# Message product: one weight block, both column halves of adj, two open accumulators

## Chip, cores, metric

The kernel runs on one NeuronCore of a Trainium2 chip. The metric is the device time of one execution in microseconds; lower is better. Three executions of the kernel before took 1776.67, 1779.15 and 1781.03 us; the median, 1779.15, is the time before.

## What is computed

The input is x, 16 graphs of 1024 nodes with 128 features, and one adjacency matrix adj of 1024 by 1024 that holds zeros and ones. Layer 0 is graph attention with a layer norm; layer 1 is a gated graph network of five steps with a layer norm. The part that matters here is the step of layer 1, cut from the reference:

```python
def step(h, _):
    m_in = jnp.einsum('nm,bmd->bnd', in_matrix, h)    # in_matrix = out_matrix = adj
    m_out = jnp.einsum('nm,bmd->bnd', out_matrix, h)
    av = jnp.concatenate([m_in, m_out], axis=-1)
    u3 = h @ u3_w.T + u3_b
    z = jax.nn.sigmoid(av @ w3_w.T + w3_b + u3)
    r = jax.nn.sigmoid(av @ w4_w.T + w4_b + u3)
    hv = jnp.tanh(av @ w5_w.T + w5_b + (r * h @ u5_w.T + u5_b))
    h = (1.0 - z) * h + z * hv
    return (h, None)
```

Both matrices are adj, so the kernel computes the message m = adj @ h once for each graph and step and folds the two halves of each weight into one (`wm`).

## The kernel before

Everything of layer 1 is held transposed: 128 features on the partitions, 1024 nodes along the row. A row of 1024 is handled in two halves of 512 (`HALF`)[...].

The message product is `s1` (lines 395 to 415). It multiplies the node states, in chunks of 128 nodes, with the rows of adj. The state `hN` is kept as the sum of two float32r tiles (index w, a rounded part and the rest), so 8 chunks times 2 parts give 16 terms for each half. The state is the weight (stationary) operand, a block of 128 by 128; adj is the moving operand, 512 columns. For half 0 all 16 terms accumulate into one bank `pm`, ScalarE copies it to SBUF as `m` (line 413), then the same 16 weight blocks are gone through again for half 1 with the other bank. That makes 32 matmuls on line 405 and two copies for each graph and step, and 16 x 5 = 80 graph steps in all.

The gates follow in `s2`: for each half one matmul with u3 (`pu`, line 423), one for r and one for z (`pr`, `pz`, line 428), each a float32 matmul that TensorE runs in two passes, with additions on VectorE and sigmoids on ScalarE. `s3` computes the candidate (`pv`, lines 443 and 444), tanh on ScalarE and the update on VectorE. `s4` transposes the new state (`pt_h`, line 255) and splits it into the two parts of `hN` (lines 459 and 460). Layer 0 is `f1` to `f4`; its line 365 uses adj and the same pool of accumulators, as `po`.

The graphs are interleaved by hand. A loop over k runs, in this order, the gates of unit k-1, the product of unit k, the candidate of unit k-1, the transposes of unit k-2 and one part of layer 0; so another unit's matmuls stand between a product and the gates that read it. The framework places the instructions on each engine's queue by the order of the source, as a planner that works with estimated times sees them ready, and adds the semaphores; the order in the trace can therefore differ from the source. Each engine then runs its queue in order.

PSUM has eight banks: two in `ps_acc` (used by `pm` and `po`), four in `ps_g` (gates), two in `ps_t` (transposes).

A second network for an adj that isn't zeros and ones is compiled in and skipped in these runs.

Of the kernel before, what the change touches and what calls it, by code (L numbers as in the profile page):

```python
# [8 lines left out]
F32 = mybir.dt.float32  # L9
# [6 lines left out]
P = 128  # L16
N = 1024
HALF = 512
NC = N // P
# [7 lines left out]
def kernel(  # L27
# [41 lines left out]
    nc = tc.nc  # L69
# [61 lines left out]
    def network(binary, pools):  # L131


        def pool(name, bufs, space=None):
            kw = {} if space is None else {"space": space}
            return pools.enter_context(tc.tile_pool(name=f"{name}{int(binary)}", bufs=bufs, **kw))
# [14 lines left out]
        ps_acc = pool("ps_acc", 2, PS)  # L151
# [114 lines left out]
        h0T, hT, hN, y0 = {}, {}, {}, {}  # L266
# [128 lines left out]

        def s1(b, s):
            m = []
            for half in range(2):
                pm = ps_acc.tile([P, HALF], F32, tag="acc", name=f"pm_{b}_{s}_{half}")
                if binary:  # L400
                    terms = [(hN[b][:, w, c, :], c) for c in range(NC) for w in range(2)]
                else:
                    terms = [(hN[b][:, c, :], c) for c in range(NC)]
                for i, (lhs, c) in enumerate(terms):
                    nc.tensor.matmul(  # L405
                        pm,
                        lhs,
                        adj[:, c, half * HALF : (half + 1) * HALF],
                        start=(i == 0),
                        stop=(i == len(terms) - 1),  # L410
                    )
                mt = mp.tile([P, HALF], F32, tag="m", name=f"m_{b}_{s}_{half}")
                nc.scalar.copy(mt, pm)  # L413
                m.append(mt)
            S[b, s] = {"m": m}

# [61 lines left out]
        for k in range(-5, last + 3):  # L478
            at(s2, k - 1)
            at(s1, k)  # L480
            at(s3, k - 1)
            at(s4, k - 2)
            b, phase = divmod(k + 5, 5)
            if b < B:
                stage_ = (f1, None, f2, f3, f4)[phase]
                if stage_ is not None:
                    stage_(b)
            if binary and 20 <= k < 20 + NC:
                look_at(k - 20)
            if binary and k == 20 + NC:  # L490
                find_flag()
# [54 lines left out]
```

## Time and profile before

| what | value |
|---|---|
| median of three executions | 1779.15 us |
| profiled span | 1776.1 us |
| TensorE matmul busy | 1694.1 us, 95% |
| VectorE busy | 1069.2 us, 60% |
| ScalarE busy | 823.1 us, 46% |
| matmul records of line 405 | 2560, 653.6 us busy |
| weight loads of line 405 | 2560, 481.4 us busy |
| copies of line 413 | 160, 580 ns each |

PE is TensorE's matmuls, PEld its weight loads, which can run beside a matmul; DVE is VectorE, ACT ScalarE, POOL GpSimd. Busy time is the time in which at least one instruction of the row was open. Matmuls are pipelined: the record of one is its latency, longer than the distance from its start to the next one's start. A row's last column is the idle time of the engine just ahead of these instructions, with what ended it after the arrow.

### The profile page before, as it was taken

What the parts mean: (1) busy time and instruction counts of PE and PEld (TensorE: products, weight loads), DVE (VectorE), ACT (ScalarE), POOL (GpSimd) and SP (SyncE); (2) the same over time, 40 slices, a digit from 0 to 9 for tenths busy, and PEclk for the clock granted to TensorE, in tenths of its full rate; (3) what the DMA queues carried; (4) which work ended last, traced back from release to release, by engine and by line L of the source; (5) the groups of instructions that cost most, each with busy time, mean ns of one, the idle gap of its engine ahead of it and who ended that gap; (6) DMA issues with size and microseconds to landing.
All of it is one profiled execution on the core that took longest, in us unless ns stands there. A gap on an engine that the chain in (4) does not pass through costs nothing.

```text
span 1776.1 us, 17218 instructions
## 1 busy us (share of the span) xinstructions
PE 1694.1 (95%) x6212; PEld 1053.3 (59%) x6212; DVE 1069.2 (60%) x2486; ACT 823.1 (46%) x1430; POOL 243.6 (14%) x196
## 2 busy tenths in 40 slices
PE   3689999999999999999999999999999999999995
PEld 2445666666666666666666666566666666666562
DVE  4586464746656475665747656474675747565555
ACT  3146363554636345463634546354463634544442
POOL 3640101102020020201002010110202001020101
PEclk8799999999999999999999999999999999999998
DMA  5110000000000000000000000000000000000000
GB/s 170 48 48 1 13 1 12 12 13 12 1 12 13 12 13 13 1 13 13 13 12 12 13 1 12 13 13 12 13 1 0 13 0 13 1 12 0 13 0 25
DMA packets 22412, 27.06 MB, mean 15 GB/s; under 512 B 1328, under 2 KB 18096, under 8 KB 22320
## 3 DMA queue, kind: packets, MB, share of 16 engines
q1 hardware_dynamic: 21376, 23.27, 4.2%
q10 hardware_dynamic: 576, 2.10, 0.3%
q8 instruction: 50, 0.82, 0.2%
q0 software_dynamic: 368, 0.53, 0.1%
q14 instruction: 42, 0.34, 0.1%
HBM read 17.50 MB, written 8.39 MB: 15 GB/s over the span
## 4 chain that ended last, share of the span: by engine, by line
PE 85%; DVE 8%; POOL 3%; DMA 2%; ACT 1%; issue 1%; SPq 0%; POOLq 0%; DVEq 0%; ACTq 0%
PE pm L405 33%; PE po L365 8%; PE pz L428 7%; PE pv L444 7%; PE pu L423 7%; PE pr L428 7%; PE pv L443 7%; PE pt_h L255 2%; DVE hv L448 2%; PE ptt L276 2%; PE pe L297 2%; PE ph L343 1%; DVE hv L447 1%; PE po L357 1%; DVE hN L460 1%; POOL zero L217 1%
## 5 line engine op out<-in xcount | busy, mean ns | idle before, releaser
L405 PE MATMUL pm<-adj,hN 128*128 128x512 f32 x2560 | 653.6, 411 | 1.4 <-DVE hN L460 1.1
L405 PEld LDWEIGHTS pm<-adj,hN 128*128 128x128 f32 x2560 | 481.4, 189 | 154.0 <-issue 33.5
L447 DVE TENSOR_TENSOR hv<-hv,h1T 128x512 f32<-128x512 f32 x128 | 88.1, 688 | 293.1 <-ACT hv L446 293.1
L425 ACT ACTIVATE u<-pu,bias 128x512 f32<-128x512 f32 x160 | 109.9, 687 | 192.2 <-PE pu L423 187.5
L430 DVE TENSOR_TENSOR r<-pr,u 128x512 f32<-128x512 f32 x160 | 108.5, 678 | 135.8 <-PE pr L428 124.0
L413 ACT COPY m<-pm 128x512 f32<-128x512 f32 x160 | 91.4, 580 | 196.4 <-PE pm L405 196.4
L444 PE MATMUL pv<-r,u 128*128 128x512 f32 x320 | 163.7, 594 | 7.5 <-DVE r L433 7.5
L446 ACT ACTIVATE hv<-pv,b 128x512 f32<-128x512 f32 x160 | 110.1, 688 | 125.8 <-PE pv L444 125.6
L428 PE MATMUL pz<-m,wm 128*128 128x512 f32 x320 | 167.4, 605 | 0.2 <-DVE r L430 0.2
L443 PE MATMUL pv<-m,wm 128*128 128x512 f32 x320 | 162.9, 592 | 1.4 <-DVE r L430 1.4
L428 PE MATMUL pr<-m,wm 128*128 128x512 f32 x320 | 163.6, 593 | 0.0
L431 ACT ACTIVATE r<-r,bias 128x512 f32<-128x512 f32 x160 | 114.5, 716 | 99.2 <-DVE r L430 99.1
L350 POOL TENSOR_TENSOR h<-full,h 128x512 fp32r<-128x512 f32 x32 | 40.5, 1265 | 795.3 <-ACT h L349 795.3
L431 ACT ACTIVATE z<-z,bias 128x512 f32<-128x512 f32 x160 | 115.2, 720 | 67.8 <-DVE z L430 66.1
L365 PE MATMUL po<-att,h 128*128 128x512 f32 x256 | 115.7, 604 | 24.8 <-DVE h L344 24.8
L423 PE MATMUL pu<-h1T,u 128*128 128x512 f32 x256 | 130.9, 593 | 0.0
L448 DVE TENSOR_TENSOR hv<-hv,z 128x512 f32<-128x512 f32 x160 | 116.8, 737 | 2.3
L430 DVE TENSOR_TENSOR z<-pz,u 128x512 f32<-128x512 f32 x160 | 109.0, 681 | 2.4 <-PE pz L428 2.3
L444 PEld LDWEIGHTS pv<-r,u 128*128 128x128 f32 x320 | 60.1, 189 | 83.1 <-issue 65.2
L451 POOL TENSOR_TENSOR h1T<-h1T,h0T 128x512 f32<-128x512 f32 x32 | 45.4, 1418 | 440.9 <-DVE h1T L449 414.9
L428 PEld LDWEIGHTS pz<-m,wm 128*128 128x128 f32 x320 | 55.6, 189 | 80.7 <-issue 36.6
L365 PEld LDWEIGHTS po<-att,h 128*128 128x128 f32 x256 | 49.3, 194 | 87.3 <-issue 78.4
(105 smaller groups left out, 2012.0 us busy)
## 6 DMA issues: line engine op xcount, KB each, us to landing
xt<-in_x_dram SPq DMA_DIRECT2D x16, 512.0 KB, 3.2
out_dram<-o SPq DMA_DIRECT2D x16, 512.0 KB, 3.2
look<-in_adj_dram SPq DMA_DIRECT2D x8, 512.0 KB, 3.3
a<-in_adj_dram ACTq DMA_DIRECT2D x4, 512.0 KB, 4.3
a<-in_adj_dram SPq DMA_DIRECT2D x4, 512.0 KB, 3.5
w<-in_L_gnn_w_w_dram POOLq DMA_DIRECT2D x3, 128.0 KB, 7.5
u<-in_L_gnn_u_w_dram POOLq DMA_DIRECT2D x2, 64.0 KB, 7.7
wot<-L_gnn_others_weight_dram SPq DMA_DIRECT2D x1, 64.0 KB, 3.3
```

The source lines that it names most:

```text
L365: nc.tensor.matmul(po, lhs, rhs, start=False, stop=(i == len(terms) - 1))
L405: nc.tensor.matmul(pm, lhs, adj[:, c, half * HALF : (half + 1) * HALF], start=(i == 0), stop=(i == len(terms) - 1),)
L423: nc.tensor.matmul(pu, u3, h, start=True, stop=True)
L425: nc.scalar.activation(u, pu, AF.Identity, bias=bias[:, 3:4], scale=1.0)
L428: nc.tensor.matmul(pg, wm[:, j, :], st["m"][half], start=True, stop=True)
L430: nc.vector.tensor_tensor(g, pg, u, ALU.add)
L431: nc.scalar.activation(g, g, AF.Sigmoid, bias=bias[:, j : j + 1], scale=1.0)
L443: nc.tensor.matmul(pv, wm[:, 2, :], st["m"][half], start=True, stop=False)
L444: nc.tensor.matmul(pv, u5, st["r"][half], start=False, stop=True)
L446: nc.scalar.activation(hv, pv, AF.Tanh, bias=b5, scale=1.0)
L447: nc.vector.tensor_tensor(hv, hv, h, ALU.subtract)
L448: nc.vector.tensor_tensor(hv, hv, st["z"][half], ALU.mult)
```

## The change

The two loops of `s1` change places. Both accumulators are taken at the start; for each of the 16 weight blocks the matmul for half 0 is followed at once by the one for half 1, and the two copies come after all 32 matmuls. It is meant to let two matmuls in a row use one weight block. The number of matmuls and copies, their shapes and the order in which each accumulator sums its terms stay the same.

```diff
         def s1(b, s):
             m = []
-            for half in range(2):
-                pm = ps_acc.tile([P, HALF], F32, tag="acc", name=f"pm_{b}_{s}_{half}")
-                if binary:
-                    terms = [(hN[b][:, w, c, :], c) for c in range(NC) for w in range(2)]
-                else:
-                    terms = [(hN[b][:, c, :], c) for c in range(NC)]
-                for i, (lhs, c) in enumerate(terms):
+            pms = [ps_acc.tile([P, HALF], F32, tag="acc", name=f"pm_{b}_{s}_{h}") for h in range(2)]
+            if binary:
+                terms = [(hN[b][:, w, c, :], c) for c in range(NC) for w in range(2)]
+            else:
+                terms = [(hN[b][:, c, :], c) for c in range(NC)]
+            for i, (lhs, c) in enumerate(terms):
+                for half in range(2):
                     nc.tensor.matmul(
-                        pm,
+                        pms[half],
                         lhs,
                         adj[:, c, half * HALF : (half + 1) * HALF],
                         start=(i == 0),
                         stop=(i == len(terms) - 1),
                     )
+            for half in range(2):
                 mt = mp.tile([P, HALF], F32, tag="m", name=f"m_{b}_{s}_{half}")
-                nc.scalar.copy(mt, pm)
+                nc.scalar.copy(mt, pms[half])
                 m.append(mt)
             S[b, s] = {"m": m}
```

## The prediction

> **What bounds the kernel now.** I read the busy rows first, then the stretches, then who waits for whom on TensorE, then the order of time around one message product.
>
> ```profile
> PE 1694.1 (95%) x6212; PEld 1053.3 (59%) x6212; DVE 1069.2 (60%) x2486; ACT 823.1 (46%) x1430; POOL 243.6 (14%) x196
> ```
>
> TensorE (PE) has work 95% of the span, and no other engine is above 60%. Cut into stretches (columns: length, busy us and instruction counts of PE, PEld, DVE, ACT, POOL, then granted clock, DMA share, GB/s):
>
> ```profile
> 0.00:100.00 100.00, 51.43 (x164) 31.47 (x165) 55.25 (x151) 29.10 (x55) 47.05 (x37) 0.80 0.30 102
> 200.00:1690.00 1490.00, 1486.15 (x5482) 926.53 (x5482) 904.69 (x2096) 716.95 (x1244) 162.84 (x138) 1.00 0.03 9
> 1690.00:1776.00 86.00, 64.79 (x224) 38.08 (x222) 44.99 (x102) 30.15 (x48) 9.52 (x8) 0.92 0.05 13
> ```
>
> In the middle 1490 us TensorE idles 3.9 us, at full granted clock. The idle is at the ends: 48.6 us in the first 100, 21.2 us in the last 86. So in the middle the time is the number of matmuls times their pace, and nothing else; removing waits there can bring at most those 3.9 us. The list of TensorE's waits for the middle stretch says the same: its largest entry is 2.1 us.
>
> The row to change is the largest of that engine:
>
> ```profile
> L405 PE MATMUL pm<-adj,hN 128*128 128x512 f32 x2560 | 653.6, 411 | 1.4 <-DVE hN L460 1.1
> L405 PEld LDWEIGHTS pm<-adj,hN 128*128 128x128 f32 x2560 | 481.4, 189 | 154.0 <-issue 33.5
> L413 ACT COPY m<-pm 128x512 f32<-128x512 f32 x160 | 91.4, 580 | 196.4 <-PE pm L405 196.4
> ```
>
> Its mean of 411 ns is a latency, since matmuls overlap; the pace has to come from starts. In order of time (start, length, engine):
>
> ```profile
> 788.49 1.02 PE L428 MATMUL pz<-m,wm 128*128 128x512 f32 x2
> ...
> 788.95 7.83 PE L405 MATMUL pm<-adj,hN 128*128 128x512 f32 x31
> ...
> 793.32 0.59 ACT L413 COPY m<-pm 128x512 f32<-128x512 f32 x1 [0.64 <-PE pm L405]
> ...
> 796.62 1.02 PE L443 MATMUL pv<-m,wm 128*128 128x512 f32 x2
> ...
> 796.81 0.59 ACT L413 COPY m<-pm 128x512 f32<-128x512 f32 x1 [2.29 <-PE pm L405]
> ...
> 797.47 1.02 PE L444 MATMUL pv<-r,u 128*128 128x512 f32 x2
> ```
>
> From pv to the next pv is 797.47 - 796.62 = 0.85 us for two passes; the records show 429 ns per pass of a float32 matmul. From the start of pz to pv is 8.13 us; less two such passes, 7.27 us are left for 31 matmuls of pm: **234 ns each**. The single records alternate between 231 and 236. At 234 ns the 2560 matmuls take 599 us, a third of the span.
>
> **What the Trainium skill says.** "TensorE: Matmul & The Clock Gate", section Back-to-back issue gap, gives N/2.4 + 2.5 ns, so 216 ns for 512 columns at full clock and 427 ns at half. The trace agrees at half clock (the first pm matmuls, at 78 us, start 427 ns apart) but not at full: pm takes 18 ns more than the page says. The same page, Step-by-step: what each phase is for, says weight loads run ahead beside the running matmul through their own read port. The trace agrees: each load starts 3 ns after the matmul before it and takes 188 ns of the 234. "PSUM — Partial Sum Buffer", The four PSUM rules, says that an accumulation group's first matmul clears the marks of its own bank only; so two open groups in two banks leave each other alone. No run here shows two open.
>
> **The change, part by part.**
>
> *Loads.* The reorder puts two matmuls with one weight block next to each other. Each call still carries its own weights. Does the second load vanish? The nearest thing in the trace is line 357, where both halves use wsi one after the other: its group has 64 matmul passes and 64 weight loads, none saved. Those are float32 passes, two for each matmul, so it is not proof for pm, where the weight is one pass. I take 2560 loads, as now. The other end: 1280 loads fewer.
>
> *Pace.* If the loads stay, does a repeated weight or a change of bank alter 234 ns? A bank change costs nothing now: between matmul 16 and 17 of a unit, where the bank changes, starts are 231 to 236 ns apart as elsewhere, and from the last pm into pv it is 232. The 18 ns over the page's pace have two readings. One is the load: then a vanished load would bring its matmul to 214.5 ns (half of 429), 19.5 x 1280 = 25.0 us. The other is the moving operand: pe on line 297 reads every second element, so as many bytes per ns as pm, and its passes start 450 ns apart against 429 of the other float32 ones. It has the same 21 ns more with a load like theirs, which speaks for the moving side, and that is unchanged. I take **0** for the pace; the ends are -25.0 us and, for the 231/236 alternation settling on either value, 2.5 x 2560 = 6.4 us each way.
>
> *Copies.* Now the first copy runs while the second half multiplies (793.32 above, 3.3 us ahead of the end). Afterwards both banks finish 0.23 us apart and the two copies of 0.59 us follow each other at the end, done some 1.3 us after it. Behind them on ScalarE stands tanh for pv, which is released only after four passes, 1.72 us; TensorE meanwhile has four pv pairs, 3.43 us, and eight transposes, 0.87 us. Over the 80 units, the first pr starts a median of 5.1 us after the last pm. The copy is hidden: 0 us. In a few units ScalarE is late with the second copy, up to 3.4 us after the product's end; those units have pr at 5.0 us. First copy done at about 4.0, second at 4.6: still in time, by less than 1 us.
>
> *Banks.* Both accumulators must be free when the product begins. In the trace the next pm starts 4.6 us or more after the one before (median 10.4), and the copies need 1.3. Line 365's accumulators, of the same pool, are followed by 2.6 us or more of gate matmuls. 0 us.
>
> *hN.* Each of its 16 blocks is wanted every 467 ns instead of 234 during the first pass over them, so a product that starts before its second group is written waits less. TensorE waits for hN in L405 for 1.4 us in the whole span, 0.2 in the middle: at most -1 us.
>
> *The ends.* The last unit has nothing between the product and pr:
>
> ```profile
> 1743.31 6.58 PE L405 MATMUL pm<-adj,hN 128*128 128x512 f32 x27
> ...
> 1746.89 0.59 ACT L413 COPY m<-pm 128x512 f32<-128x512 f32 x1 [2.72 <-PE pm L405]
> ...
> 1749.72 1.02 PE L428 MATMUL pr<-m,wm 128*128 128x512 f32 x2
> ```
>
> Here pr must wait for a copy that ended 2.2 us earlier before: now +0.7 us (0.59 plus handing over). Two units early and late in the run start pr 0.71 us after the product; there the copy just arrives. Sum of the ends +0.7 to +1.5, less up to 1 for hN: **+0.5 us**, so 1779.15 + 0.5 = 1779.7, which I round to 1780.
>
> **Rivals.**
> (a) *The loads or their cost go.* -25.0 us: **1754 us**. For: loads are 59% of the span in records, and the pace over the page's is real. Against: line 357 keeps its loads, and line 297's same surplus points to the moving operand.
> (b) *The late copies become a wait.* Slower. If each of the 80 products exposed one copy, 80 x 0.59 = 47 us: 1826 us. If only in those units where ScalarE stands behind a cast that waits for a layer norm (some 13 of the middle stretch), 13 x 1 us: **1792 us**. For: ScalarE's queue is in order, and the program's order on TensorE is not the source's (one pm stands alone between pu and pr at 787.00), so a planner may place things anew and less well. Against: 5.1 us of other work against 1.3 us of copies.
> (c) *The pace shifts by the alternation alone.* 1773 or 1786 us.
>
> **How the numbers follow.** No measurable change 0.56, at 1780, between 1775 and 1784. Faster 0.17: 0.11 for (a), 0.06 for the small end of (c). Slower 0.27: 0.18 for a few exposed waits up to 1795 (with the upper end of (c)), 0.09 for more. The range 1768 to 1795 leaves out 0.11 below and 0.09 above.
>
> **What would show it.** In the changed profile the L405 weight-load row has x2560 and about 189 ns, and L405 matmuls still start 234 ns apart (busy near 653 us). A count near 1280, or starts near 215 ns for every second one, would prove (a). ScalarE's copies stand in pairs at the end of each product, their wait for pm is longer in one piece, and TensorE's idle in 200 to 1690 stays under 6 us. If pr or pm gains idle time with the copy as its releaser, (b) is right. If the middle idle stays small but the busy time of L405 has moved, my step on the pace is wrong.

## The result, and the profile after

| kernel | median, us | lowest to highest | runs |
|---|---|---|---|
| before | 1778.07 | 1776.67 to 1781.03 | 4 |
| changed | 1785.70 | 1784.76 to 1787.20 | 4 |

The ratio is 1.0042, 95% interval [1.0024, 1.0059]: 7.6 us slower. The time lies in the forecast range, but on its slower side, outside the main case, and most of the loss has one cause.

The page of the changed kernel, the rows that answer to those of before (line 413 is now 414, and pz has moved from 428 to 429):

```profile
PE 1699.4 (95%) x6212; PEld 1054.4 (59%) x6212; DVE 1070.1 (60%) x2486; ACT 822.7 (46%) x1430; POOL 243.8 (14%) x196
...
L405 PE MATMUL pm<-adj,hN 128*128 128x512 f32 x2560 | 653.5, 411 | 1.3 <-DVE hN L461 1.1
L405 PEld LDWEIGHTS pm<-adj,hN 128*128 128x128 f32 x2560 | 481.7, 189 | 153.8 <-issue 30.6
...
L414 ACT COPY m<-pm 128x512 f32<-128x512 f32 x160 | 85.2, 584 | 205.4 <-PE pm L405 205.4
L429 PE MATMUL pz<-m,wm 128*128 128x512 f32 x320 | 168.0, 607 | 3.8 <-DVE r L431 3.8
```

The product itself is untouched: 2560 matmuls, 2560 weight loads, 653.5 us busy against 653.6. Neighbouring starts inside it are 233.4 ns apart in the mean of the stretch from 200 to 1690 us, as before. What is new is in the last row: pz now waits for VectorE, 3.8 us in all, where it waited 0.2 before.

The list of TensorE's waits in the stretch from 200 to 1690 us (total, number, longest), first the rows of the changed kernel that matter here:

```profile
PE pz L429 <- DVE r L431: 3.8, 14, 0.3
PE pt_y L255 <- DVE hN L461: 2.1, 13, 0.2
```

and then that of pz before:

```profile
PE pz L428 <- DVE r L430: 0.2, 1, 0.2
```

One of the 14 waits, near 1665 us, is the one that stood there before. The other 13 are new: one for each graph of this stretch, about 105 us apart. Here is one such place in order of time, first in the changed kernel, TensorE and VectorE:

```profile
328.35 1.02 PE L429 MATMUL pr<-m,wm 128*128 128x512 f32 x2
328.42 0.63 DVE L241 BATCH_NORM_AGGREGATE mv_b<-stats_b 128x2 f32<-128x6 f32 x8
...
328.96 0.66 DVE L431 TENSOR_TENSOR r<-pr,u 128x512 f32<-128x512 f32 x1
...
329.68 1.12 PE L429 MATMUL pz<-m,wm 128*128 128x512 f32 x2 [0.31 <-DVE r L431]
```

and the same place before:

```profile
328.68 0.62 DVE L241 BATCH_NORM_AGGREGATE mv_b<-stats_b 128x2 f32<-128x6 f32 x8
329.12 1.02 PE L428 MATMUL pr<-m,wm 128*128 128x512 f32 x2
329.22 0.66 DVE L430 TENSOR_TENSOR r<-pr,u 128x512 f32<-128x512 f32 x1
...
329.97 1.09 PE L428 MATMUL pz<-m,wm 128*128 128x512 f32 x2
```

Two passes of pr take 0.86 us, so pz is due at 328.35 + 0.86 = 329.21 in the changed kernel and starts at 329.68: 0.47 us late. (The view says 0.31, because the record of pr, a latency, reaches 0.16 us past the time at which the next matmul could start.) Before, it was due at 329.98 and started at 329.97; the addition it needs had ended at 329.88, only 0.10 us ahead. In the changed kernel, where pz does wait, it starts 0.06 us after the addition's end (329.62), so only about 0.04 of that 0.10 us was to spare. The place had almost no slack, and nothing in the list of waits showed it, because a wait that is just met leaves no entry.

What has pz to do with an addition to r? It reads only m and wm, nothing that the addition writes. But the gate matmuls take the four banks of `ps_g` in turn (a bank is one of the accumulators in PSUM), and a unit makes them in the order pu, pr, pz, pu, pr, pz; so the second pz takes the bank of the first pr, and must wait until the addition has read it.

Why is the addition later against TensorE? Follow VectorE back: the addition stands behind a layer norm's statistics and the state update, which start from tanh on ScalarE. ScalarE there, changed:

```profile
319.44 0.72 ACT L432 ACTIVATE z<-z,bias 128x512 f32<-128x512 f32 x1 [0.58 <-DVE z L431]
320.07 0.70 ACT L432 ACTIVATE r<-r,bias 128x512 f32<-128x512 f32 x1
320.70 0.72 ACT L432 ACTIVATE z<-z,bias 128x512 f32<-128x512 f32 x1
321.32 1.05 ACT L414 COPY m<-pm 128x512 f32<-128x512 f32 x2
322.27 0.70 ACT L447 ACTIVATE hv<-pv,b 128x512 f32<-128x512 f32 x1
```

and before:

```profile
319.51 0.58 ACT L413 COPY m<-pm 128x512 f32<-128x512 f32 x1
320.19 0.72 ACT L431 ACTIVATE z<-z,bias 128x512 f32<-128x512 f32 x1
320.81 0.71 ACT L431 ACTIVATE r<-r,bias 128x512 f32<-128x512 f32 x1
321.44 0.72 ACT L431 ACTIVATE z<-z,bias 128x512 f32<-128x512 f32 x1
322.07 0.57 ACT L413 COPY m<-pm 128x512 f32<-128x512 f32 x1
322.54 0.69 ACT L446 ACTIVATE hv<-pv,b 128x512 f32<-128x512 f32 x1
```

Before, the first copy filled the 0.6 us in which ScalarE waited for VectorE ahead of z. Now that time is idle (the 0.58 in brackets), and both copies stand between the last sigmoid and tanh. The first tanh starts a median of 2.52 us after the first pv, against 2.04 before, and the addition ends 9.87 us after it, against 9.38, over 14 such places, of which 13 are late. There pz is late by 5.9 us in all (0.1 before), which is nearly all of the 6.4 us that the stretch from 200 to 1690 lost. Between these two times the instructions of TensorE (the order of the halves within a product apart) and of VectorE run in the same order in both traces; of the three, only ScalarE's queue is ordered anew. Most of the rest is at the end: the last unit adds 1.3 us, and its pr starts 0.43 us after the product's end where it started 0.17 us ahead of it.

### The profile page after: what moved, and what is told of

Read it like the earlier page. It is cut to its first block, busy times and chain, and to the rows that moved or that the text cites. A ratio compares the mean times of both kernels' runs of the same rounds, so it can differ in the third digit from the quotient of the medians.

```text
span 1782.9 us, 17219 instructions
## 1 busy us (share of the span) xinstructions
PE 1699.4 (95%) x6212; PEld 1054.4 (59%) x6212; DVE 1070.1 (60%) x2486; ACT 822.7 (46%) x1430; POOL 243.8 (14%) x196
## 5 line engine op out<-in xcount | busy, mean ns | idle before, releaser
L405 PE MATMUL pm<-adj,hN 128*128 128x512 f32 x2560 | 653.5, 411 | 1.3 <-DVE hN L461 1.1
L414 ACT COPY m<-pm 128x512 f32<-128x512 f32 x160 | 85.2, 584 | 205.4 <-PE pm L405 205.4
```

Source lines behind the costliest of these rows:

```text
L405: nc.tensor.matmul(pms[half], lhs, adj[:, c, half * HALF : (half + 1) * HALF], start=(i == 0), stop=(i == len(terms) - 1),)
```

## The experiments

**Theory T** is the chain just read: both halves finish together, so the first copy moves behind three sigmoids in ScalarE's queue; tanh is 0.48 us later; VectorE, in order, is later; a gate matmul waits for a bank that VectorE must empty. **Theory R**: the matmul order itself costs something, through alternating banks, repeated weights or two open accumulators. The ratios below are to the kernel before, timed again beside each group of runs, with medians of 1776.8 to 1777.0 us. The cuts of code are against the changed kernel or the kernel before, as each text says; `...` stands for lines left out.

**Both halves late, nothing shared.** The order of the kernel before, with one matmul moved to the end; the edit is in the changed kernel:

```diff
-            for i, (lhs, c) in enumerate(terms):
-                for half in range(2):
+            n = len(terms)
+            order = [(0, i) for i in range(n - 1)] + [(1, i) for i in range(n)] + [(0, n - 1)]
+            for half, i in order:
+                    lhs, c = terms[i]
```

> Order of the kernel before (15 terms of half 0, then all of half 1), except that the last term of half 0 comes at the very end. No weight block is shared by neighbouring matmuls and banks do not alternate, but both halves finish together, and on ScalarE the first copy stands behind z, r and z of the unit before, as in the changed kernel. Theory T (the late first copy delays tanh on ScalarE, VectorE's in-order queue passes it on to the gate addition, and a gate matmul waits for that addition's bank, about 0.47 us once a graph, 13 times): slower than before by about 6 us, near 1785; the pz matmul waits for the r addition some 13 times. Theory R (alternating banks or repeated weights cost something by themselves): as before, 1778.

Measured: 1784.46 us, ratio 1.0045 [1.003, 1.0059]. The waits of its TensorE have the new row:

```profile
PE pz L431 <- DVE r L433: 3.6, 13, 0.3
```

So the loss comes without alternating and without neighbouring equal weights, and R isn't needed for it. Half 0 finishing late is enough.

**Other weights side by side.** The changed kernel, with half 1 two terms ahead:

```diff
-            for i, (lhs, c) in enumerate(terms):
+            for i in range(len(terms)):
                 for half in range(2):
+                    lhs, c = terms[(i + 2 * half) % len(terms)]
```

> The changed kernel with the two banks alternating, but half 1 two terms ahead of half 0, so that neighbouring matmuls never have the same weight block. If a repeated block has any value (or cost) for the pace, line 405's starts move from 234 ns: by 19 ns on half of the matmuls at most, 24 us. Theory T: the same pace of 234 ns, the same time as the changed kernel, 1785 plus or minus 1.5, and 2560 loads.

Measured: 1784.97 us, ratio 1.0042 [1.0028, 1.0056], 2560 loads, and a median of 234 ns between starts. A repeated weight block shows neither gain nor cost here.

**Finish early, but how early?** Two kernels share the first blocks and then finish half 0, then half 1. They differ in one number, 2 or 4 shared blocks. Of the edit in the changed kernel, the order with 2:

```diff
...
+            order = [(h, i) for i in range(2) for h in range(2)] + [(h, i) for h in range(2) for i in range(2, n)]
...
```

> Both accumulators open from the start; the first two weight blocks are shared by both halves, then the other 14 terms of half 0, then those of half 1. The first copy stands right behind the casts of hN on ScalarE, ahead of z, r, z, as in the kernel before. Theory T: as before, 1778 plus or minus 1.5, with no pz waits of 0.3 us. A theory that two open banks as such delay something: nearer 1785.

> As e2_share_first_2, with four shared blocks: half 0 is still done 12 matmuls (2.8 us) ahead of half 1, but on ScalarE the planner puts the first copy behind the first z, so that it no longer fills the idle time ahead of z. Theory T: about as slow as the changed kernel, 1783 to 1786, though the copy's data are ready 2.8 us ahead. If it is only the time at which half 0 finishes, not the place in ScalarE's queue: as before, 1778.

Measured: 1776.56 us with two, ratio 0.9998 [0.9989, 1.0006]; 1782.10 us with four, ratio 1.0033 [1.0022, 1.0043], a little under the expected 1783 to 1786. ScalarE with two shared blocks:

```profile
318.00 0.58 ACT L416 COPY m<-pm 128x512 f32<-128x512 f32 x1
318.68 0.72 ACT L434 ACTIVATE z<-z,bias 128x512 f32<-128x512 f32 x1
```

and with four:

```profile
319.65 0.72 ACT L434 ACTIVATE z<-z,bias 128x512 f32<-128x512 f32 x1 [0.58 <-DVE z L433]
320.28 0.56 ACT L416 COPY m<-pm 128x512 f32<-128x512 f32 x1
```

With four, half 0 is done 12 matmuls, 2.8 us, ahead of half 1, and that doesn't help: the copy is queued behind one z instead of ahead of it, the 0.58 us ahead of z are idle again, and the pz waits are back (against one of 0.2 us with two):

```profile
PE pz L431 <- DVE r L433: 3.1, 13, 0.3
```

The two traces show TensorE's instructions (the halves within a product apart) and VectorE's in the same order from beginning to end, the order of the kernel before. So it is the place in ScalarE's queue that costs, as T says. The planner sets that place from its estimates.

**More of the suspected cost, on the kernel before.** The second copy is made twice:

```diff
                 nc.scalar.copy(mt, pm)
+                if half:
+                    nc.scalar.copy(mt, pm)
```

> The kernel before, unchanged in its matmuls, but the second copy of each unit is made twice in a row on ScalarE (the same result). It puts 0.58 us more ahead of tanh. Theory T: the slot that was just in time becomes late, 0.4 to 0.6 us for each of 13 graphs and a little at the ends, so +5 to +8 us, near 1784, with pz waiting for the r addition 13 times. If the changed kernel's loss came from its matmul order and not from ScalarE's queue: as before, 1777.

Measured: 1784.04 us, ratio 1.0043 [1.0029, 1.0057], with these waits:

```profile
PE pz L430 <- DVE r L432: 5.1, 14, 0.4
```

The source leaves the matmuls as before. The planner moved some of TensorE's and VectorE's instructions, so more than one thing differs, but the chain is the one of T: the first tanh starts 2.63 us after the first pv, the addition ends at 9.98, and pz is 0.54 to 0.57 us late in 12 of the 13 graphs and 0.42 in the other. One more copy of 0.58 us ahead of tanh makes the loss.

**The same copies, on another queue.** The changed kernel with one edit:

```diff
-                nc.scalar.copy(mt, pms[half])
+                if half:
+                    nc.vector.tensor_copy(mt, pms[half])
+                else:
+                    nc.scalar.copy(mt, pms[half])
```

> The changed kernel with the second copy of each unit on VectorE instead of ScalarE. ScalarE then reaches tanh one copy sooner, and VectorE makes the copy in the 1.5 us in which it waits for tanh. Theory T: the waits of pz vanish, 1777 to 1779. If both banks finishing late is what costs, whoever copies: 1785.

Measured: 1779.60 us, ratio 1.0016 [1.001, 1.0023], a little over the expected 1777 to 1779. ScalarE reaches tanh after one copy:

```profile
320.22 0.57 ACT L417 COPY m<-pm 128x512 f32<-128x512 f32 x1
320.69 0.69 ACT L450 ACTIVATE hv<-pv,b 128x512 f32<-128x512 f32 x1
```

The 13 waits are gone (one of 0.2 us is left), and tanh and the addition are back at 2.04 and 9.39 us after the first pv. Some 2.8 us above before remain, and the trace shows where most of them arise. Once a graph, near 261 us for the first time, the planner put the first pm of a product behind pr and pz instead of ahead of them. There the weight load of pz waits for ScalarE's u; pz starts 0.08 us late, and its second pass comes 0.10 us later still (533 instead of 429 ns after the first). Over 13 graphs that makes 2.4 us, in pieces too short for the list of waits.

**Another bank for pz.** The changed kernel, with pu in the transposes' banks:

```diff
-                pu = ps_g.tile([P, HALF], F32, tag="g", name=f"pu_{b}_{s}_{half}")
+                pu = ps_t.tile([P, 4, P], F32, tag="t", name=f"pu_{b}_{s}_{half}").rearrange("p j n -> p (j n)")
```

> The changed kernel, with pu (line 424) in the two transpose banks instead of the four gate banks. The second pz of a unit then has a gate bank of its own and need not wait for the addition of the first r. Theory T with the bank as its last link: the 13 waits of pz vanish, back to 1777 to 1779, unless the transposes now wait for pu's bank. If the wait of pz is not for a bank: 1785 as the changed kernel.

Measured: 1801.88 us, ratio 1.0144 [1.0128, 1.0159], slower than either value expected. Its waits:

```profile
PE pv L445 <- DVE r L434: 12.9, 13, 1.0
PE pu L424 <- DVE hN L461: 9.6, 13, 0.8
```

The waits of pz are gone, as they should be if a bank was their reason, but pu now waits for VectorE to empty a transpose bank, and the planner ordered TensorE's instructions anew. In the changed kernel a pu stands between the transposes and the last pv of some units; here it doesn't (at 362.60 us, for one), so that pv comes sooner to the multiplication of r by h on VectorE, which itself waits 2.04 us for ScalarE's sigmoid, and pv waits 1.00 us. With several things moved at once this run agrees with the last link of T and does not prove it; that link rests on the order of the banks in the kernel.

**What makes the pace 234 ns?** Two changes to the changed kernel, each for the pace of line 405 only; neither computes the whole product. The first halves most weight loads:

```diff
+                    q = slice(0, P if i in (0, len(terms) - 1) else 64)
...
-                        pms[half],
-                        lhs,
+                        pms[half][q, :],
+                        lhs[:, q],
```

> For the pace of line 405 alone. 14 of the 16 weight blocks of each half are 64 columns instead of 128, so the weight load is half as long; the moving operand is as in the changed kernel. Left out: these terms for features 64 to 127. If the 18 ns over 216 are caused by the weight load beside the matmul: about 225 ns. If by the moving operand: 234 ns.

The second reads one column of adj over and over:

```diff
-                        adj[:, c, half * HALF : (half + 1) * HALF],
+                        adj[:, c, half * HALF : half * HALF + 1].to_broadcast([P, HALF]),
```

> For the pace of line 405 alone. The moving operand is one column of adj, read 512 times, so the weight load is as in the changed kernel and the moving stream reads one address. Left out: the true columns of adj in the product. If the 18 ns come from reading 2 KB per partition at this speed: near 216 ns. If from the load, or from the number of reads whatever they touch: 234 ns.

Measured: with half loads, a load record of 135 ns instead of 188 (medians) and starts 233 ns apart (median; means over the middle stretch 232.2 against 233.4). Its row of loads, whose mean of 142 ns takes in the loads of 128 columns:

```profile
L406 PEld LDWEIGHTS pm<-adj,hN 128*64 128x64 f32 (+1 forms) x2560 | 363.1, 142 | 269.2 <-issue 29.0 <-DVE hN L462 6.9 <-ACT hN L461 4.6
```

With one column, starts are 216 ns apart. Two rows of its matmuls:

```profile
L405 PE MATMUL pm<-adj,hN 128*128 128x512 f32 x2560 | 609.6, 395 | 1.0 <-DVE hN L461 0.8 <-ACT hN L460 0.2
L429 PE MATMUL pz<-m,wm 128*128 128x512 f32 x320 | 168.0, 607 | 10.6 <-DVE r L431 10.6
```

So the surplus of 18 ns is in reading the moving operand: a load that takes 53 ns less brings about 1 ns. Sharing weights, which drops no load here anyway, had next to nothing of the 18 ns to win. The second row is a warning: with TensorE faster by 44 us in line 405, the slot at pz that was just met before came to 10.6 us of waiting. The times, of one execution each, were 1781.34 and 1749.63 us.

**A version from this.** If the bytes of the moving operand count, fewer bytes help. The kernel before, in its own order, with its three float32r tiles in bfloat16:

```diff
...
-        adj = tables.tile([P, NC, N], F32R if binary else F32, tag="adj", name="adj")
+        adj = tables.tile([P, NC, N], BF16 if binary else F32, tag="adj", name="adj")
...
-                return hnp.tile([P, 2, NC, P], F32R, tag="hN", name=name)
+                return hnp.tile([P, 2, NC, P], BF16, tag="hN", name=name)
...
-                h2 = l0.tile([P, 2, NC, P], F32R, tag="h2", name=f"h2_{b}")
+                h2 = l0.tile([P, 2, NC, P], BF16, tag="h2", name=f"h2_{b}")
```

> The kernel before, in its own order, with adj (zeros and ones, exact) and the two parts of hN and of h on line 365 in bfloat16 instead of float32r. [...] The moving operand has half the bytes. From the run with one column: if the bytes read set the 18 ns, 2560 + 256 matmuls fall from 234 to 216 ns, 51 us less, near 1726; since the slots in which a gate matmul is just in time become late when TensorE gets faster, 5 to 15 us of it come back, so 1731 to 1741. If bfloat16 brings the pace but not the time, VectorE or ScalarE bound the middle: above 1760.

Measured: 1733.85 us, ratio 0.9759 [0.9746, 0.9773], faster than both kernels by 43 us or more. It is no free gain: the state is carried by two 2-byte parts in place of two 4-byte ones, and no run here puts a number on what that costs in exactness. Starts are 216 ns apart. Its rows:

```profile
L405 PE MATMUL pm<-adj,hN 128*128 128x512 bf16 x2481 | 556.8, 380 | 5.1 <-DVE hN L460 1.6
L405 PEld LDWEIGHTS <-hN 128*128 128x128 bf16 x2560 | 250.1, 98 | 334.8 <-issue 42.4 <-DVE hN L460 10.4 <-ACT hN L459 4.9
```

(79 of the matmul records are missing from this trace.) The loads are shorter too, 98 ns; the run with half loads says that this is not what counts. The two runs at 216 ns complete each other: the one-column run keeps the type, this one keeps the true columns of adj. Both fit a limit on the bytes read; no run changes the number of bytes alone. Of the 51 us that the pace gives, 43 arrive. Most of what is missing is the slot of pz again: the list of waits of its middle stretch has 12 of pz for r, and pz starts 4.8 us late in all there, over 13 graphs.

## Why the prediction was right and where it was not

**The number** lies inside 1768 to 1795, but the main case, no measurable change between 1775 and 1784, did not come. What came is the case of a few exposed waits, which had 0.18. That the range held is owed to its width and not to the account of the copies. The sign given for the middle stretch failed too: TensorE is idle there for 7.5 us, not under 6.

**Loads: right.** 2560 before and after, as line 357 had suggested. **Pace: right**, 0 taken and 0 measured, with the interval between 231 and 236 as it was; and of the two readings of the surplus, the one that line 297 spoke for was confirmed. (Its "as many bytes per ns as pm" holds only if the bytes that are stepped over count as read.) **Banks and hN: right.** The product's own waits stayed at 1.3 us, and no pm waited for a copy in the middle. The Trainium skill, "PSUM — Partial Sum Buffer", The four PSUM rules, says that a group's first matmul clears the marks of its own bank only. The trace doesn't test that rule; it shows that two groups open side by side in two banks ran at the old pace of 233.4 ns. **Ends: right in kind**: the last pr is 0.6 us later against its product, for 0.7 forecast.

**The step that failed is "Copies", whose term was 0 and should have been about 5.9 us.** It named tanh as what stands behind the copies, and then let tanh have 1.72 us from the end of the product. That holds for a ScalarE that is free at the end of the product. The same paragraph says that ScalarE is up to 3.4 us late in a few units, and checks only pr against that, on TensorE. For those units it was tanh that counted: 13 graphs, each with tanh 0.48 us later, passed on through VectorE's queue to a bank that pz had been getting with about 0.04 us to spare. Rival (b), in its limited form of 13 x 1 us, had the units and the reason, ScalarE behind a cast that waits for a layer norm; its size was about twice too large, since one copy of 0.58 us moved, not a wait of 1 us. It also looked for the copy itself as the releaser; the list names VectorE's addition, which stands behind a tanh and a row of VectorE's instructions. Only the last pr waits for a copy, 0.4 us.

The sign that was read wrongly is the small waits. 3.9 us of idle time in 1490 said that waits could not be removed with profit. It does not say that they can't be added: pz was met with about 0.04 us to spare once a graph.

## What to carry to other kernels

A tuned pipeline with one saturated engine may show almost no waits and still have no slack: before moving a release later, take the places where the saturated engine needs it and measure by how much each is met, not only whether it waits. On an in-order engine, follow every instruction behind the moved one to its last consumer, and above all where that engine already runs late. Before sharing weights, see whether the loads bound the pace and whether a shared one is really dropped. Here all 2560 stayed, and the reading of the moving operand set the pace; a moving operand of half the bytes brought 43 us.

## What the runs showed of the hardware

The pace of 512-column matmuls at full clock depends on how the moving operand is read. In these runs it is 234 ns with float32r, 216 ns with the same type from one column read over and over, 216 ns with bfloat16, and 233 ns with float32r and half the weight columns. The formula of the Trainium skill, "TensorE: Matmul & The Clock Gate", Back-to-back issue gap, gives 216 ns, as the gap of a matmul by itself and without regard to type; that agrees with the bfloat16 run and not with the run that reads all columns in float32r, where the measurement decides. At a granted clock of 0.50, at 78 us in the kernel before, float32r starts are 427 ns apart, twice 213.5, so the surplus doesn't show there.
